# One PSUM tile for both halves in layer 0's mixers, and the ranks' diagonals written during the ranking

## The chip, the cores and the metric

The kernel runs on one core of a Trainium2 chip. The metric is the device time of one execution in microseconds, as the median of several runs; lower is better. The engines are called PE (matmuls; PEld are its weight loads), ACT, DVE, POOL and SP. The queues of SP, ACT and POOL also issue the DMA transfers; a transfer issued by SP is shown under "SPq".

## The reference

The network is a "metaformer" of four layers on a batch of 4 images of 64 channels, 128 x 128. Only two of its stages matter here.

Layer 0's mixer works on each of the 256 channel images ("tokens") on its own. Cut to what matters:

```python
an = _inorm(a, n2_g, n2_b)
h = gelu(_inorm(_spectral_conv(an, m1_spec, (H, W))) + _conv1x1(an, m1_sw, m1_sb))
h = _inorm(_spectral_conv(h, m2_spec, (H, W))) + _conv1x1(h, m2_sw, m2_sb)
o = _inorm(h, mo_g, mo_b) + a
```

`_spectral_conv` takes a two-dimensional Fourier transform, keeps 32 x 17 low modes, multiplies them by weights and transforms back; `_inorm` normalises one image. The input `a` of the mixer is itself partly made of low modes, which an earlier part of the layer has left in memory.

Layer 1's attention replaces a 128 x 128 score matrix of each of 256 tokens by a function of the rank of each score in its matrix:

```python
tau = jnp.argsort(-flat, axis=-1)
ranks = (jnp.argsort(tau, axis=-1) + 1).astype(score.dtype) / n
weights = -jnp.log(ranks).reshape(shp)
```

The score is a negated squared distance, so the matrix is symmetric and its diagonal is zero, the largest value: the diagonal's ranks are known beforehand.

## The kernel before

**Layer 0's mixers** (`l0_mixer`). 256 images are taken as 16 blocks of NB = 16 images, two groups `g` of eight blocks; up to DEEP = 3 blocks are under way at once. The steps of a block are not issued where they are written: each is a `step(engine, us, reads, writes, fn, new=..., late=...)` of a `Plan`, which knows how many buffers each name has and, at `emit`, picks the next step for each engine by the costs `us` written there. PE, ACT, DVE and POOL then run in exactly that order; SP's order is left to the framework.

A block goes three times through `inverse`, the transform from modes back to the image: once for the low modes `lo` from memory (used by `add_low`), once for the modes `o` after the first weights (`conv1`), once for those after the second (`conv2`). Between them `spectral` goes the other way (`p1`, `yl`, `p2`, `m`, `o`), and `image_stats` and `root` give the normalisations.

The modes of 16 images lie as two halves of HB = 8 images on partitions 0 to 48 and 64 to 112. `inverse` takes them in two quarters, each with four images of either half:

- `over_ky`: eight matmuls into `pa`, image by image and half by half, from 49 rows to 64 partitions and 128 columns. Each half h has a PSUM tile of its own, `pa0` and `pa1`, of which it uses partitions 64h to 64h + 63; there is one buffer of each.
- `empty`: ACT brings `pa` into the SBUF tile `gt` (two buffers), half by half. For `lo` it is one copy per half (line 923); for the other two, `scaled` (line 861) takes one activation per half and image, with a scale per partition and image (`r1` or `r2`) and a bias. A scaled quarter thus has eight activations of 64 partitions x 128 elements.
- `over_kx`: two matmuls, one per half, from the 64 partitions of `gt` to all 128 partitions of `pb0` and `pb1`, 512 columns each. In the trace each matmul of fp32 data appears as two instructions, so a quarter has 16 for `pa` and 4 for `pb`.
- DVE takes `pb` in (`add_low`, lines 967 and 982).

A block ends with the residual tiles `xt`, loaded by SP, and a store of `zz` by POOL (line 1031).

**The diagonals.** Two DRAM tensors `pk`, one per group of 128 tokens, hold the ranks: 128 x 16384 int32, 8 MiB each. Their diagonals come from a constant matrix of 16384 numbers, whose other elements are written over later. The function `diagonals` issues one DMA per group on POOL's queue, which spreads the constant over all 128 tokens. It is handed into the mixers as `aside` and is a POOL step of the second block of group 1, behind that block's `lo`.

**The ranking** (`l1_ranks`). The 8128 pairs above the diagonal are sorted by a merge network of 91 stages, for two groups of 128 tokens in turn. In the forward pass (`sort_stage`) ACT copies the lower keys, POOL subtracts, ACT takes the sign into a mask `turned`, SP writes the mask to DRAM, and DVE takes minimum and maximum of two half-stages. The pass back (`back_stage`) reads the masks and undoes the network on the positions. `finish` then writes the ranks into `pk`, 127 DMAs on SP per group (line 1565), and `l1_blocks` reads them.

Of the kernel before, what the change touches and what calls it, by code (L numbers as in the profile page):

```python
# [10 lines left out]
F32 = mybir.dt.float32  # L11
# [5 lines left out]
AF = mybir.ActivationFunctionType  # L17
# [5 lines left out]
P = 128  # L23
B, H, W, C = 4, 64, 128, 128
NI = B * H
KR = 49
# [22 lines left out]
class Plan:  # L49
# [16 lines left out]
    def step(self, engine, us, reads, writes, fn, new="", late=0.0):  # L66

        i, deps, holds = len(self.steps), set(), []
        for n in new.split():

            self.last[n] = [set(), None, set()]
            self.users.append((n, self.last[n][0]))
            holds.append(len(self.users) - 1)
            if n in self.turns:
                self.turns[n].append(holds[-1])
        for n in reads.split():
            t = self.last[n]
            t[0].add(i)
            if t[1] is not None:
                deps.add(t[1])  # L80
            t[2].add(i)
        for n in writes.split():
            t = self.last.setdefault(n, [set(), None, set()])
            t[0].add(i)
            deps |= t[2]
            if t[1] is not None:
                deps.add(t[1])
            t[1], t[2] = i, set()
        for n in new.split():
            self.last[n][0].add(i)  # L90
        deps.discard(i)
        self.steps.append((engine, us, deps, holds, fn, late))
# [190 lines left out]
    return s  # L283


def l0_conv(env, x, out, tscr, prm, cst, aside):


    nc, tc = env.nc, env.tc
    KCH = ((0, 11), (11, 22), (22, 32))  # L290
    with ExitStack() as ctx:
# [8 lines left out]
        fx = const(cp, "fx", [P, 192])  # L300
        sc = {}
# [10 lines left out]
        mix = [cp.tile([P, P], F32, name="at2_%d" % g) for g in range(2)]  # L312

        tk0 = cp.tile([P, W, C], F32, name="tk0")
# [4 lines left out]
        modes = [dram.tile([KR, 64, P], F32, name="modes%d" % g) for g in range(2)]  # L319
        with ExitStack() as mctx:  # L320
# [4 lines left out]
            psum = pool("l0ps", 2, space=PSUM)  # L325
# [113 lines left out]
            with tc.tile_pool(name="l0w", bufs=1) as wp:  # L439
# [9 lines left out]
                for k in "qkv":  # L449
                    w = wp.tile([8, 16, 9, 2], F32, name="w_" + k)  # L450
# [3 lines left out]
                for k, d, dst in (("q", dqk[0], wqk[0]), ("k", dqk[1], wqk[1])):  # L454
                    t = wp.tile([8, 2, 144], F32, name="t_" + k)
# [42 lines left out]
                t0 = wp.tile([8, 1], F32, name="t0")  # L498
# [139 lines left out]
        k = {n: const(cp, n, s) for n, s in (  # L638
            ("ex", [P, W]), ("ey", [KH, C]), ("fk", [P, 2, 2, 64]), ("gw", [KH, 32]), ("first", [P, 1]),
            ("sides", [KH, P]))}  # L640
        for n in ("m1", "m2"):
            for r in range(2):
                w = cp.tile([KH, 32], F32, name="%s_w%d" % (n, r))
# [25 lines left out]
        k["c0"] = cp.tile([P, 1], F32, name="c0")  # L669
        nc.vector.tensor_add(k["c0"], sc["an_b"], sc["mo_b"])  # L670

        l0_mixer(env, x, out, tscr, mix, modes, fx, k, sc, tk0, aside)


def l0_mixer(env, x, out, tscr, mix, modes, fx, k, sc, y0, aside):

# [5 lines left out]
    with tc.tile_pool(name="l0y", bufs=1) as yp, tc.tile_pool(name="l0m", bufs=DEEP) as sb, tc.tile_pool(name="l0s", bufs=DEEP) as sm, tc.tile_pool(  # L684
        name="l0mp", bufs=2, space=PSUM
    ) as psum, tc.tile_pool(name="l0mq", bufs=1, space=PSUM) as ps1:
        plan = Plan(dict(
            gate=DEEP, xt=3, lo=2, z=DEEP, yl=1, m=1, o=DEEP, sq=1, gt=2, p1=2, p2=1, pa=1, pb=1,
            **{n: DEEP for n in (
                "st", "d", "mu", "red", "small", "ka", "kb", "kn", "kc", "va", "knh", "v1", "r1", "b1", "ks", "r2", "g2",  # L690
                "t",
# [130 lines left out]
        def inverse(v, name, modes_of, put, put_us, reads, use, use_us, uses, writes, new=""):  # L822


            def quarter(t0):
                w = {}

                def over_ky():
                    w["pa"] = [ps1.tile([P, 4, C], F32, name="pa%d" % h) for h in range(2)]
                    for j in range(4):  # L830
                        for h in range(2):
                            q = 64 * h
                            T.matmul(
                                w["pa"][h][q : q + 64, j, :], modes_of(q, t0 + j), k["ey"][q : q + KR], start=True, stop=True
                            )

                def empty():
                    w["gt"] = sb.tile([P, 4, C], F32, name="gt", bufs=2)
                    for h in range(2):
                        put(64 * h, t0, w["gt"], w["pa"][h])  # L840

                def over_kx():
                    w["pb"] = [ps1.tile([P, 4, C], F32, name="pb%d" % h) for h in range(2)]
                    for h in range(2):
                        q = 64 * h
                        T.matmul(w["pb"][h], k["ex"][q : q + 64], w["gt"][q : q + 64], start=True, stop=True)

                step("pe", 2.0, name, "pa", over_ky, new="pa")
                step("act", put_us, "pa " + reads, "gt", empty, new="gt")
                step("pe", 3.0, "gt", "pb", over_kx, new="pb")  # L850
                for h in range(2):
                    step("dve", use_us, "pb " + uses, writes(t0), lambda h=h: use(h * HB + t0, w["pb"][h]),
                         new=new if t0 == h == 0 else "")

            for t0 in range(0, HB, 4):
                quarter(t0)

        def scaled(scale, bias):
            def put(q, t0, gt, pa):
                for j in range(4):  # L860
                    S.activation(
                        gt[q : q + 64, j, :], pa[q : q + 64, j, :], AF.Identity, bias=bias(q, t0 + j),
                        scale=scale()[q : q + 64, t0 + j : t0 + j + 1],
                    )
            return put

# [35 lines left out]
        def block(g, y, made, s0, par):  # L902
# [9 lines left out]
                    nc.sync.dma_start(v["lo"][64 * h : 64 * h + KR], modes[g][:, :, s0 + HB * h : s0 + HB * h + HB])  # L912

            step("sp", 0.2, "", "lo", load_modes, new="lo gate", late=4.0)
            if g == 1 and s0 == NB:
                step("pool", 2.0, "lo", "", aside)

            def add_low(t0, pb):
                V.tensor_add(yt[:, t0 : t0 + 4, :], yt[:, t0 : t0 + 4, :], pb)

            inverse(
                v, "lo", lambda q, t: v["lo"][q : q + KR, :, t],
                lambda q, t0, gt, pa: S.copy(gt[q : q + 64], pa[q : q + 64]), 1.2, "",
                add_low, 0.75, " ".join(made), lambda t0: "l%d" % t0,
            )
            tag1, v1 = spectral(v, lambda: yt, lambda j: "l%d" % (j % HB), "m1", 4, par)
# [36 lines left out]
            def conv1(t0, pb):  # L963
# [7 lines left out]

            inverse(
                v, "o", lambda q, t: v["o"][q : q + KR, t, :],
                scaled(lambda: v["r1"], lambda q, t: v["b1"][q : q + 64, t : t + 1]), 3.6, "r1 b1",
                conv1, 1.4, "l0 l4 ks", lambda t0: "z", new="z",
            )
            step("act", 3.4, "", "z", lambda: S.activation(v["z"], v["z"], AF.Gelu))
# [3 lines left out]
            def conv2(t0, pb):  # L981
# [3 lines left out]

            inverse(
                v, "o", lambda q, t: v["o"][q : q + KR, t, :],
                scaled(lambda: v["r2"], lambda q, t: k["b2"][q : q + 64]), 3.6, "r2",
                conv2, 0.75, "", lambda t0: "z",
            )  # L990
            tagz, var2 = image_stats(v, lambda: v["z"], 2, "z", par)
# [461 lines left out]
def l1_ranks(env, dscr, keys, pk, masks, ties, tables):  # L1453
# [9 lines left out]
    with ExitStack() as ctx:  # L1463
# [175 lines left out]
        with tc.tile_pool(name="low", bufs=2, space=PSUM) as lows, tc.tile_pool(  # L1639
            name="diff", bufs=4  # L1640
        ) as diffs, tc.manual_schedule(engines={E.Activation, E.DVE, E.Pool}):
            for i in range(ns):
                for g in range(2):
                    sort_stage(g, i)
        spare = ctx.enter_context(tc.tile_pool(name="spare", bufs=1)).tile([P, NSORT], F32, name="spare")
        for g in range(2):
            number(g, keys[g], spare)
# [1738 lines left out]
def metaformer(tc, a, out, cst):  # L3386

    with ExitStack() as ctx:
        env = Env(ctx, tc)
        nc = tc.nc  # L3390
        dp = ctx.enter_context(tc.tile_pool(name="dram", bufs=1, space=DRAM))
        state = [dp.tile([NI, W, C], F32, name="state%d" % i) for i in range(5)]
        tokens = dp.tile([NI, W, C], F32, name="tokens")
        dist = dp.tile([NI, W * W], F32, name="dist")

        pk = [dp.tile([P * W * W, 1], I32, name="pk%d" % g) for g in range(2)]
        masks = [dp.tile([P, sum(NSORT // (2 * p) * (p - k if k < p else p) for p, k in merge_network(NSORT))], I8,
                         name="masks%d" % g) for g in range(2)]
        def part(prefix):
            return {k[len(prefix) :]: v for k, v in a.items() if k.startswith(prefix)}  # L3400

        x = a["x"].rearrange("b h w c -> (b h) w c")
        f0, f2 = part("L0_ffn_"), part("L2_ffn_")

        def diagonals():
            for g in range(2):
                nc.gpsimd.dma_start(
                    pk[g][0 : P * W * W, :].rearrange("(t f) o -> t (f o)", t=P), cst["l1c_diag"].partition_broadcast(P)
                )

        l0_conv(env, x, state[0], tokens, part("L0_conv_"), cst, diagonals)
        rnn_ffn(env, state[0], state[1], f0["W"], f0["VT"], f0["gamma"], f0["beta"])
        l1_layer(
            env, state[1], state[2], dist, pk, masks, part("L1_conv_"), part("L1_ffn_"), {"rowend": cst["l1c_rowend"]}
        )
        l2_conv(env, state[2], state[3], part("L2_conv_"))
        rnn_ffn(env, state[3], state[4], f2["W"], f2["VT"], f2["gamma"], f2["beta"])
        l3_layer(env, state[4], out.rearrange("b h w c -> (b h) w c"), part("L3_conv_"), part("L3_ffn_"))
# [36 lines left out]
```

## Time and profile before

| | us |
|---|---|
| runs, median of 3 | 11948.84 |
| runs, lowest and highest | 11933.74, 11949.30 |
| the profiled execution | 11937.16 |
| its span, first to last instruction | 11935.4 |
| layer 0 before the mixers | 0 to about 500 |
| the mixers | about 500 to 1420 |
| layer 0's feed-forward part | 1420 to about 1780 |
| distances of layer 1 | 1780 to about 2045 |
| ranking, forward pass | 2045 to about 3600 |
| ranking, pass back and `finish` | to 5334 |
| the rest of layer 1, layers 2 and 3 | to the end |

The stages are cut where the first instruction of the next begins on the queue that loads for it. A "busy" time of an engine is the union of its instructions' times; the idle time before an instruction is put down to what released it. The rows of PE are modelled at their ends, so a busy PE need not be at its peak. Over the whole span DVE is busy 84%, ACT 63%, PE 61% and POOL 52%, but these are averages over stages with different limits.

### The profile page before, as it was taken

What the parts mean: (1) busy time and instruction counts of PE and PEld (TensorE: products, weight loads), DVE (VectorE), ACT (ScalarE), POOL (GpSimd) and SP (SyncE); (2) the same over time, 40 slices, a digit from 0 to 9 for tenths busy, and PEclk for the clock granted to TensorE, in tenths of its full rate; (3) what the DMA queues carried; (4) which work ended last, traced back from release to release, by engine and by line L of the source; (5) the groups of instructions that cost most, each with busy time, mean ns of one, the idle gap of its engine ahead of it and who ended that gap; (6) DMA issues with size and microseconds to landing.
All of it is one profiled execution on the core that took longest, in us unless ns stands there. A gap on an engine that the chain in (4) does not pass through costs nothing. (4 is left out here: it accounts for less than half of the span.)

```text
span 11935.4 us, 113939 instructions
## 1 busy us (share of the span) xinstructions
PE 7337.1 (61%) x33966; PEld 4454.9 (37%) x33966; DVE 10014.6 (84%) x16358; ACT 7522.4 (63%) x10863; POOL 6182.3 (52%) x5276
## 2 busy tenths in 40 slices
PE   7887796000000000009998899989999999998665
PEld 5665564000000000008886344444444444446443
DVE  7566637999999999988996899999999999996444
ACT  4255534888867777633332778777878787875332
POOL 1000016999970000002332899998999999994222
PEclk8876798555555555559999899999999999999887
DMA  4223245111111111121111343433333334333434
GB/s 139 89 43 100 63 149 140 56 57 58 58 56 54 55 54 56 49 49 42 47 45 35 129 143 140 144 135 137 135 140 139 143 138 143 139 133 117 169 131 152
DMA packets 632396, 1193.48 MB, mean 100 GB/s; under 512 B 216556, under 2 KB 433998, under 8 KB 552398
## 3 DMA queue, kind: packets, MB, share of 16 engines
q1 hardware_dynamic: 587550, 1043.02, 26.1%
q0 software_dynamic: 34656, 140.92, 3.6%
q8 instruction: 274, 4.49, 0.2%
q10 hardware_dynamic: 9552, 2.08, 0.1%
q14 instruction: 364, 2.98, 0.1%
HBM read 950.89 MB, written 251.71 MB: 101 GB/s over the span
## 5 line engine op out<-in xcount | busy, mean ns | idle before, releaser
L2717 POOL TENSOR_TENSOR gs<-hist,cc 128x512 f32<-128x512 f32 x2048 | 2576.5, 1266 | 378.9 <-DVE hist L2712 217.1
L2712 DVE TENSOR_TENSOR_SCAN hist<-da,state,bs 128x512 f32<-128x512 f32 x1984 | 2523.9, 1272 | 0.0
L2726 PE MATMUL py<-gs,ident 128*128 128x512 f32 x4096 | 2246.0, 631 | 5.1 <-DVE y L2602 3.7
L1633 PE MATMUL pt<-ident,both 128*128 128x128 f32 x6 | 2.7, 447 | 3258.0 <-DVE both L1631 3258.0
L2683 ACT ACTIVATE da<-dt,am 128x512 f32<-128x512 f32 x2048 | 1414.8, 715 | 325.6 <-DVE hist L2712 323.0
L2704 DVE TENSOR_TENSOR bs<-dx,bs 128x512 f32<-128x512 f32 x2048 | 1393.8, 681 | 187.7 <-PE bs L2690 143.0
L1509 POOL TENSOR_TENSOR diff<-key 128x2048 f32<-128x2048 f32 (+11 forms) x364 | 1383.8, 3861 | 86.8 <-DVE key L1514 75.2
L1633 PEld LDWEIGHTS pt<-ident,both 128*128 128x128 f32 x6 | 1.1, 183 | 3259.5 <-issue 3259.5
L2726 PEld LDWEIGHTS py<-gs,ident 128*128 128x128 f32 x4096 | 739.3, 197 | 902.5 <-issue 441.2
L1884 POOL IOTA row<- 72x1 int32 x1 | 0.1, 136 | 1800.7 <-ACTq L1833 1800.7
L2690 PE MATMUL bs<-bt,pick 96*128 96x512 bf16 x2048 | 807.3, 394 | 140.3 <-DVE hist L2712 137.3
L1531 ACT COPY keep<-rank 128x1536 int16<-128x1536 int16 (+11 forms) x364 | 612.8, 1686 | 437.9 <-DVE rank L1533 389.0
L1507 ACT COPY low<-key 128x2048 f32<-128x2048 f32 (+11 forms) x364 | 626.7, 1722 | 285.1 <-DVE key L1514 276.4
L1532 DVE COPY_PREDICATED rank<-back,rank 128x1536 int16<-128x1536 uint8 (+11 forms) x364 | 781.8, 2148 | 16.7 <-ACT keep L1531 16.7
L1533 DVE COPY_PREDICATED rank<-back,keep 128x1536 int16<-128x1536 uint8 (+11 forms) x364 | 778.0, 2137 | 12.5
L1514 DVE TENSOR_TENSOR key<-low,key 128x2048 f32<-128x2048 f32 (+11 forms) x364 | 744.5, 2045 | 12.4
L1513 DVE TENSOR_TENSOR key<-low,key 128x2048 f32<-128x2048 f32 (+11 forms) x364 | 749.2, 2058 | 6.5 <-DMA key<-dist 6.2
L1510 ACT ACTIVATE turned<-diff 128x2048 int8<-128x2048 f32 (+11 forms) x364 | 600.0, 1697 | 36.4 <-DMA key<-dist 27.6
L1522 ACT ACTIVATE back<-turned 128x3072 uint8<-128x3072 int8 (+12 forms) x182 | 582.3, 3200 | 0.0
L2183 PE MATMUL pe<-ew,xg 128*128 128x128 f32 x4096 | 504.4, 277 | 0.0
L1031 POOL DMA_DIRECT2D state<-zz x16 | 18.6, 1161 | 909.7 <-DVE zz L1021 854.5
L2183 PEld LDWEIGHTS pe<-ew,xg 128*128 128x128 f32 x4096 | 488.2, 193 | 3.9
(826 smaller groups left out, 18502.8 us busy)
## 6 DMA issues: line engine op xcount, KB each, us to landing
cc<-cd SPq DMA_DIRECT2D x512, 1024.0 KB
xt<-state SPq DMA_DIRECT2D x64, 1024.0 KB
xo<-state SPq DMA_DIRECT2D x128, 256.0 KB
state<-xo POOLq DMA_DIRECT2D x128, 256.0 KB, 2.8
xl<-in_L_ffn_weight SPq DMA_DIRECT2D x32, 1024.0 KB
tk<-in_x SPq DMA_DIRECT2D x32, 512.0 KB
tokens<-tt POOLq DMA_DIRECT2D x32, 512.0 KB, 5.2
tk<-tokens SPq DMA_DIRECT2D x8, 2048.0 KB
```

The lines of the kernel that those rows point to most:

```text
L1509: nc.gpsimd.tensor_sub(d, lo[part], hi[part])
L1513: nc.vector.tensor_tensor(lo[part], c, hi[part], ALU.min)
L1514: nc.vector.tensor_tensor(hi[part], c, hi[part], ALU.max)
L1532: nc.vector.copy_predicated(l, t, h)
L1533: nc.vector.copy_predicated(h, t, kv)
L2183: T.matmul(w["pe"][:, j, :], w["xg"][:, q, j, :], ew[:, q, :], start=False, stop=(j == 3 and q == E - 1))
L2683: nc.scalar.activation(da, x_["dt%d" % b], AF.Exp, scale=am[:, s : s + 1])
L2690: nc.tensor.matmul(bs, pick[:, s, :], x_["bt%d" % b], start=True, stop=True)
L2704: nc.vector.tensor_mul(db, x_["dx%d" % b], db)
L2712: nc.vector.tensor_tensor_scan(h, live.pop(("da", t)), live.pop(("db", t)), 0.0 if first else state[b][:, s : s + 1], ALU.mult, ALU.add,)
L2717: nc.gpsimd.tensor_tensor(gs, h, live.pop(("cc", t)), ALU.mult)
L2726: nc.tensor.matmul(x_["py%d" % b], env.ident, live.pop(("gs", t)), start=(s == 0), stop=(s == S - 1))
```

## The change

The two tiles `pa0`, `pa1` become one tile `pa` in a pool with two buffers: half h writes partitions 64h to 64h + 63 of the same tile. ACT empties all 128 partitions at once: one copy where there were two, four activations where there were eight. The plan is told so: `pa` has two buffers, and the costs of the four steps become smaller. The function `diagonals` and its step on POOL go away; the forward pass of the ranking issues the same bytes on SP, one piece of 1024 numbers for 128 tokens (0.5 MiB) after both groups' stages of each of 32 iterations in the middle, 16 pieces for one group and then 16 for the other.

```diff
@@ l0_mixer
-            gate=DEEP, xt=3, lo=2, z=DEEP, yl=1, m=1, o=DEEP, sq=1, gt=2, p1=2, p2=1, pa=1, pb=1,
+            gate=DEEP, xt=3, lo=2, z=DEEP, yl=1, m=1, o=DEEP, sq=1, gt=2, p1=2, p2=1, pa=2, pb=1,
...
                 def over_ky():
-                    w["pa"] = [ps1.tile([P, 4, C], F32, name="pa%d" % h) for h in range(2)]
+                    w["pa"] = psum.tile([P, 4, C], F32, name="pa")
                     for j in range(4):
                         for h in range(2):
                             q = 64 * h
                             T.matmul(
-                                w["pa"][h][q : q + 64, j, :], modes_of(q, t0 + j), k["ey"][q : q + KR], start=True, stop=True
+                                w["pa"][q : q + 64, j, :], modes_of(q, t0 + j), k["ey"][q : q + KR], start=True, stop=True
                             )
 
                 def empty():
                     w["gt"] = sb.tile([P, 4, C], F32, name="gt", bufs=2)
-                    for h in range(2):
-                        put(64 * h, t0, w["gt"], w["pa"][h])
+                    put(t0, w["gt"], w["pa"])
...
-                step("pe", 2.0, name, "pa", over_ky, new="pa")
+                step("pe", 1.3, name, "pa", over_ky, new="pa")
                 step("act", put_us, "pa " + reads, "gt", empty, new="gt")
-                step("pe", 3.0, "gt", "pb", over_kx, new="pb")
+                step("pe", 1.1, "gt", "pb", over_kx, new="pb")
...
         def scaled(scale, bias):
-            def put(q, t0, gt, pa):
+            def put(t0, gt, pa):
                 for j in range(4):
                     S.activation(
-                        gt[q : q + 64, j, :], pa[q : q + 64, j, :], AF.Identity, bias=bias(q, t0 + j),
-                        scale=scale()[q : q + 64, t0 + j : t0 + j + 1],
+                        gt[:, j, :], pa[:, j, :], AF.Identity, bias=bias(t0 + j), scale=scale()[:, t0 + j : t0 + j + 1]
                     )
...
-            if g == 1 and s0 == NB:
-                step("pool", 2.0, "lo", "", aside)
...
-                lambda q, t0, gt, pa: S.copy(gt[q : q + 64], pa[q : q + 64]), 1.2, "",
+                lambda t0, gt, pa: S.copy(gt, pa), 0.6, "",
...
-                scaled(lambda: v["r1"], lambda q, t: v["b1"][q : q + 64, t : t + 1]), 3.6, "r1 b1",
+                scaled(lambda: v["r1"], lambda t: v["b1"][:, t : t + 1]), 1.9, "r1 b1",
...
-                scaled(lambda: v["r2"], lambda q, t: k["b2"][q : q + 64]), 3.6, "r2",
+                scaled(lambda: v["r2"], lambda t: k["b2"]), 1.9, "r2",
@@ l1_ranks
             for i in range(ns):
                 for g in range(2):
                     sort_stage(g, i)
+                if ns // 2 - 16 <= i < ns // 2 + 16:
+                    g, q = divmod(i - ns // 2 + 16, 16)
+                    q *= P * W // 16
+                    nc.sync.dma_start(
+                        pk[g][0 : P * W * W, :].rearrange("(t f) o -> t (f o)", t=P)[:, q : q + P * W // 16],
+                        tables["diag"][q : q + P * W // 16].partition_broadcast(P),
+                    )
@@ metaformer
-        def diagonals():
-            for g in range(2):
-                nc.gpsimd.dma_start(
-                    pk[g][0 : P * W * W, :].rearrange("(t f) o -> t (f o)", t=P), cst["l1c_diag"].partition_broadcast(P)
-                )
-
-        l0_conv(env, x, state[0], tokens, part("L0_conv_"), cst, diagonals)
+        l0_conv(env, x, state[0], tokens, part("L0_conv_"), cst)
```

The argument `aside` goes from the functions that handed it on, and the table of the diagonals is handed to `l1_layer` instead.

More of the change, by code (lines that the diff above doesn't have):

```diff
@@ L283, in symmetrize, with l0_conv @@
     return s
-def l0_conv(env, x, out, tscr, prm, cst, aside):
+def l0_conv(env, x, out, tscr, prm, cst):
     nc, tc = env.nc, env.tc
@@ L670, in l0_conv, with l0_mixer @@
         nc.vector.tensor_add(k["c0"], sc["an_b"], sc["mo_b"])
-        l0_mixer(env, x, out, tscr, mix, modes, fx, k, sc, tk0, aside)
-def l0_mixer(env, x, out, tscr, mix, modes, fx, k, sc, y0, aside):
+        l0_mixer(env, x, out, tscr, mix, modes, fx, k, sc, tk0)
+def l0_mixer(env, x, out, tscr, mix, modes, fx, k, sc, y0):
     nc, tc = env.nc, env.tc
@@ L3403, in metaformer @@
         f0, f2 = part("L0_ffn_"), part("L2_ffn_")
-        def diagonals():
-            for g in range(2):
-                nc.gpsimd.dma_start(
-                    pk[g][0 : P * W * W, :].rearrange("(t f) o -> t (f o)", t=P), cst["l1c_diag"].partition_broadcast(P)
-                )
-        l0_conv(env, x, state[0], tokens, part("L0_conv_"), cst, diagonals)
+        l0_conv(env, x, state[0], tokens, part("L0_conv_"), cst)
         rnn_ffn(env, state[0], state[1], f0["W"], f0["VT"], f0["gamma"], f0["beta"])
         l1_layer(
-            env, state[1], state[2], dist, pk, masks, part("L1_conv_"), part("L1_ffn_"), {"rowend": cst["l1c_rowend"]}
+            env, state[1], state[2], dist, pk, masks, part("L1_conv_"), part("L1_ffn_"),
+            {"rowend": cst["l1c_rowend"], "diag": cst["l1c_diag"]},
         )
```

## The prediction

> **What bounds the kernel now.** Both halves of the change lie in stages far from each other, so I read the busy table by stage first, the waits and groups of each stage next, and single instructions last. The mixers of layer 0 run from about 500 to 1420 us. In the table of windows (columns: busy us and count of PE, weight loads, DVE, ACT, POOL, then the granted TensorE clock, DMA share, GB/s):
>
> ```profile
> 500.00:1420.00 920.00, 749.56 (x4056) 510.45 (x4055) 591.21 (x2164) 502.65 (x1172) 19.83 (x20) 0.72 0.26 66
> 2500.00:2800.00 300.00, 0.00 (x0) 0.00 (x0) 297.40 (x154) 243.88 (x154) 282.41 (x76) 0.50 0.14 57
> 940.00:960.00 20.00, 16.38 (x113) 13.23 (x113) 11.24 (x39) 10.73 (x28) 2.26 (x3) 0.84 0.87 236
> 960.00:980.00 20.00, 15.70 (x78) 8.12 (x74) 15.53 (x65) 7.86 (x23) 0.00 (x0) 0.67 1.04 332
> 980.00:1000.00 20.00, 18.61 (x90) 12.38 (x90) 9.38 (x32) 16.42 (x35) 0.00 (x0) 0.62 0.93 283
> ```
>
> The mixers are paced by PE: busy 750 of 920 us, no other engine over 65%. The ranking's forward pass (second line) is paced by DVE, 297 of 300 us, with the DMA engines at 14%. The last three lines are the flood of the diagonals, 16.8 MB from 949 us on.
>
> Then the waits of the mixers (engine, line, releaser: total us, times, longest), and the groups kept apart by shape:
>
> ```profile
> PEld pb L846 <- ACT gt L861: 94.2, 85, 2.9
> PE pb L846 <- ACT gt L861: 41.8, 47, 2.8
> PE pa L833 <- DVE o L802: 38.1, 13, 4.1
> L861 ACT ACTIVATE gt<-pa,b,r 64x128 f32<-64x128 f32 x512 | 191.0, 448 | 82.4 <-PE pa L833 72.3 <-DVE r L711 4.9 <-DVE r L961 3.4
> L923 ACT COPY gt<-pa 64x512 f32<-64x512 f32 x64 | 37.1, 580 | 21.8 <-PE pa L833 20.7
> ```
>
> What PE waits for most is ACT emptying `pa`. The cost is larger than the wait, as four lines of the timeline show (start, length, engine, then idle before):
>
> ```profile
> 809.03 1.97 PE L833 MATMUL pa<-ey,o 49*64 49x128 f32 x16
> 811.08 3.01 ACT L861 ACTIVATE gt<-pa,b,r 64x128 f32<-64x128 f32 x8 [3.78 <-PE pa L833]
> 812.62 3.59 PE L846 MATMUL pb<-gt,ex 64*128 64x512 f32 x4 [1.63 <-ACT gt L861]
> 799.95 2.08 PE L846 MATMUL pb<-gt,ex 64*128 64x512 f32 x4
> ```
>
> The first half's four activations release the first two `pb` matmuls at 812.62; the other two must wait 1.5 us for the second half's, and the four take 3.59 us. Where both halves were ready (799.95) the same four take 2.08 us, because the two 64-row halves run side by side.
>
> Last, the diagonals: DVE waits for a residual tile whose load is behind the flood.
>
> ```profile
> 1012.54 1.14 DVE L1008 SCALAR_TENSOR_TENSOR xt<-tk,ka,xt 128x128 f32<-128x128 f32 x4 [17.87 <-DMA xt<-in_x]
> L3407 POOL DMA_DIRECT2D pk<-in_l1c_diag x2: 545/556/566, 949.2 to 949.8; - x2
> 16.19 0.37 SPq L297 DMA_DIRECT2D ex<-in_l0c_ex  x1
> ```
>
> **What the Trainium skill says.** "TensorE: Matmul & The Clock Gate", Part 3 (packing small matmuls): matmuls on different row and column tiles of the array run concurrently. The trace agrees: the sixteen quarter-array `pa` matmuls took 1.09 us at 1344.76 where sixteen whole-array ones of the same width (`p` from `fx`, 1068.69) took 2.02. The same page, Part 1: the array's clock falls to half after some microseconds of idling; the trace shows 0.5 to 1.0 granted, and `pb` at 1.13 or 2.08 us for the same four. "PSUM — Partial Sum Buffer", the section on bank collisions: column tiles may write one bank at once on disjoint partitions; different row tiles may not share a bank at once, which is then narrowed to the same 32-partition quadrant by measurement. The new `pa` differs in both. The trace shows column tiles alone doing it: `p2` writes both halves into one bank, and its sixteen 256-wide matmuls took 2.46 us at 1064.75, about twice the 1.13 us of the four 512-wide `pb`, which are paired and have half the columns. "DMA: Bandwidth & Descriptors", on issuing engines: all queues share sixteen DMA engines and interleave; the 17.87 us above is that.
>
> **The change part by part.**
>
> *Fewer activations.* Per scaled quarter, eight 64x128 become four 128x128, each copy two 64x512 become one 128x512. The nearest row: partitions don't lengthen an ACT instruction (a 128x256 from PSUM takes 467 ns at L2625, a 128x512 copy about 580). So ACT sheds (191 + 37)/2 = 114 us, worth nothing by itself, since ACT is busy 503 of 920.
>
> *Its effect on PE.* A scaled quarter's `gt` is whole when the old first half was, so `pb` starts when it did and runs at 2.08 rather than 3.59: 1.51 us. In the timeline's `pb` rows 33 of 64 scaled quarters show 3.59, 8 more are split in two with a wait between (about as much): 41 x 1.51 = 62 us. Of the 32 plain quarters 12 show 2.67 instead of 2.07: 7 us. Sum 69. The others had cover (PE had other work), and gain nothing.
>
> *Two buffers of `pa`* (the bank count stays: two banks before, two after). The second quarter's `pa`, 1.97 us, can go into the idle time before the first quarter's `pb`. That is at most the 41.8 + 8.6 us of PE waits; the repeating pattern 1.63 + 0.68 us a block, in some 13 blocks, gives 30.
>
> *The planner's costs.* A quarter's PE steps fall from 5.0 to 2.4 us. Summing the planner's costs over one block, PE falls from 48.6 to 33 and DVE, 44, becomes what it orders by; before, PE's 48.6 stood beside a measured 54 us from one block to the next (the 3.59 us row at 1103.58 and its like at 1158.33 and 1211.43). Real DVE work is about 591/920 of that, 35 us, so DVE doesn't bind, but the order changes and some of the gain will turn into waits on DVE such as `o` (38.1 us now). I take 80% of 69 + 30: **80 us**, some 6 us a block from 54 to 48. Bounds: 20, where the order eats most of it, and 160, where a block comes near PE's own work, 54 x 750/920 = 44 less 5 for the pairs, and the clock rises with it.
>
> *The diagonals leave layer 0.* POOL loses two issues (1.1 us) between two stores, of no weight. The stall goes: DVE stood 17.87 us for that load, and a wait of 4.35 came before it. What it cost is read from the stores of `zz`: those at 948.08 and 1016.04 are 68.0 us apart, against 53 to 55 around them, so **13 us**, bounds 10 and 22 (both waits in full). The residual load is then on time; what is late next is ACT's last scaling, as in other blocks.
>
> *They arrive in the ranking.* 32 pieces of 0.5 MB, each about 2 us of the DMA engines at the 236 to 332 GB/s above, 65 us in all, over some 560 us at a share of 14%. On SP 32 issues of some 0.4 us, 13 us, on a queue that waits 1350.8 us there for ACT's `turned`. Behind them in SP's queue stand the mask stores; their release is needed only three masks later, some 25 us. Cover: DVE at 99%. **0 us**, bounds 0 and 10. The later rank writes into `pk` (254 on SP at 5175 to 5323) now follow SP's own transfers instead of POOL's, long landed: 0, bounds -2 and 5.
>
> Sum: -80 - 13 + 0 = -93 from the profiled execution's 11937.2 (span 11935.4 and 1.8 around it) is 11844. The runs shown have a median of 11948.8 and reach down to 11933.7; the profiled one is near their lower end, so I add 6: **11850 us**.
>
> **Rivals.**
>
> *The pieces don't stay in the ranking.* SP's order isn't written out by hand; the last line of the last fence shows a constant asked for after the attention going out at 16.19 us, half a millisecond ahead of its place. The pieces need nothing in SBUF and wait for nothing, so they could go out at the start too. There 20 MB move in 120 us; 16.8 more at about 300 GB/s makes 124 us of transfers: cost between 0 and 56, take 30. Against it: the loads seen that early are of the same stage. Time 11880. Chance 0.25.
>
> *The gain becomes another wait.* The new order leaves PE waiting for `o`, `red` or the gelu; half or less of the 80 comes, say 35: 11895. For: those waits sum to over 70 us now. Against: DVE has a third of its time free. Chance 0.12.
>
> *Slower: one bank makes the two halves' `pa` matmuls take turns.* Then sixteen take as long as unpaired ones: 0.96 us more at full clock, 1.9 at half; 96 quarters x 1.4 = 137, less 93, +44: 11937 + 6 + 44 = 11987. It decides from 93/96 = 0.97 us a group on. For: the skill's sentence on row tiles. Against: the halves are in different quadrants, and `p2` pairs in one bank. Chance 0.08.
>
> **How the numbers follow.** My forecast has 0.55. About 0.2%, 24 us, is what a measurement can tell from no change. Faster: 0.55 + 0.25 and a bit under half of the third case, 0.84; same 0.07; slower 0.09, the bank and a little for an order that turns out badly. The range runs from the upper bounds of both gains, nearly (160 + 13 is 11770), to the early flood at its full 56 with 70% of the gain in order (11925); outside are the bank and a few extremes.
>
> **What would show it.** L861 256 times at 128x128 near 450 ns; `pb` in fours at 1.1 to 2.1 us without 3.59; stores of `zz` 47 to 49 us apart and no stall near 949; PE's waits for `gt` under half. The pieces on SP between about 2400 and 3100 us with DVE still at 99%. I am wrong if `pa` groups of sixteen last over 3 us, if the pieces show in the first 100 us, or if PE's waits for DVE grow by what the waits for ACT lose.

## The result and the profile after

| | before | after |
|---|---|---|
| median of 5 runs each, us | 11948.84 | 11887.27 |
| lowest and highest, us | 11932.91, 11949.59 | 11861.20, 11917.43 |
| the profiled execution, us | 11937.16 | 11887.27 |

The ratio after/before is 0.9954, with a 95% interval from 0.9937 to 0.9971: about 61 us less by the medians, 50 us less by the profiled executions. The forecast was 93 less. So the sign and the range held, and between half and two thirds of the gain came: the forecast's own ratio, 11850 to the 11943 that it started from, is 0.9922, which lies below the measured interval.

The table of windows of the kernel after shows the mixers and the ranking (columns as before: busy us and count of PE, weight loads, DVE, ACT, POOL, then clock, DMA share, GB/s):

```profile
500.00:1420.00 920.00, 674.72 (x4315) 501.94 (x4315) 618.23 (x2302) 413.64 (x944) 26.53 (x37) 0.77 0.22 54
2500.00:2800.00 300.00, 0.00 (x0) 0.00 (x0) 297.47 (x149) 244.44 (x149) 286.36 (x75) 0.50 0.14 58
```

PE's busy time in the mixers' window fell from 750 to 675 us and ACT's from 503 to 414. But the mixers end only some 47 us sooner, so the window of the kernel after holds some 50 us of the next stage too: PE shed more work than the time did. In the ranking the DMA share and the throughput stand where they stood. That is the first surprise, since 32 pieces were to pass there.

The waits of the mixers (engine, what it waited in, releaser: total us, times, longest) name the second surprise:

```profile
PEld pb L844 <- ACT gt L859: 73.2, 25, 14.7
PE pb L844 <- ACT gt L859: 66.5, 16, 14.5
PE pa L832 <- DVE o L801: 32.3, 9, 4.9
```

PE's wait for `gt` was to halve. It grew from 41.8 to 66.5 us, in a third of the times: 47 short waits, 2.8 us at most, became 16, one of them 14.5 us long. The groups kept apart by shape show that the merging itself did what the diff says:

```profile
L859 ACT ACTIVATE gt<-pa,b,r 128x128 f32<-128x128 f32 x256 | 94.8, 464 | 57.2 <-PE pb L844 28.8 <-DVE r L956 19.9 <-DVE r L710 8.6
L844 PE MATMUL pb<-gt,ex 64*128 64x512 f32 x384 | 173.9, 811 | 88.3 <-ACT gt L859 66.5 <-DVE zz L962 14.3 <-DVE zz L977 5.7
```

Before, the second of these rows read:

```profile
L846 PE MATMUL pb<-gt,ex 64*128 64x512 f32 x384 | 233.6, 923 | 51.5 <-ACT gt L861 41.8 <-ACT gt L923 8.6 <-DVE kn L942 1.1
```

There are half as many activations, each 464 ns where a half took 448, and `pb` keeps PE busy for 174 us where it was 234: 60 us of PE gone.

For what follows, a stage table helps. It is read from single rows: the last store of `modes` by POOL (the end of what stands before the mixers), and the first and last store of `zz` after it.

| kernel | `modes` end | first `zz` store | last `zz` store | mixers (last store less `modes` end) |
|---|---|---|---|---|
| before | 484.9 | 618.4 | 1413.6 | 928.8 |
| after | 493.1 | 672.6 | 1366.2 | 873.1 |

The 49.9 us of the profiled executions are 55.7 from the mixers, less 8.2 lost ahead of them, and 2.4 over the rest of the program.

### The profile page after: what moved, and what is told of

Its sections match the earlier page's. It is cut to its first block, busy times and chain, and to the rows that moved or that the text cites. A ratio compares the mean times of both kernels' runs of the same rounds, so it can differ in the third digit from the quotient of the medians.

```text
span 11885.4 us, 113599 instructions
## 1 busy us (share of the span) xinstructions
PE 7219.7 (61%) x33966; PEld 4411.3 (37%) x33966; DVE 10015.2 (84%) x16358; ACT 7406.1 (62%) x10575; POOL 6180.0 (52%) x5274
## 3 DMA queue, kind: packets, MB, share of 16 engines
q8 instruction: 273, 4.47, 0.2%
q10 hardware_dynamic: 9552, 2.08, 0.1%
```

## The experiments

Each time is compared with the kernel before as it was measured beside it, since the median of before alone went from 11919 to 11949 us. A mixers' time comes from one profiled execution. Where two kernels have the same order in the mixers and no flood there, these times differ by 3 us (after and the fourth run) and 5 us (third and ninth), and the fifth run lies 13 us from the sum of its parts; so a single step of 10 us or less is not read from them.

**First: the merged tile alone, in the old order.** The costs stay as before, the plan counts one buffer of `pa`, and the diagonals stay on POOL. (`pa=1` or `pa=2` is what the plan reckons with; the pool of the merged tile has two buffers in every run.) In the traces PE and DVE then run the same instructions in the same order as before in the mixers. Against the kernel after, beside the diagonals:

```diff
-  pa=2, pb=1,
+  pa=1, pb=1,
-  step("pe", 1.3, name, "pa", over_ky, new="pa")
+  step("pe", 2.0, name, "pa", over_ky, new="pa")
-  step("pe", 1.1, "gt", "pb", over_kx, new="pb")
+  step("pe", 3.0, "gt", "pb", over_kx, new="pb")
-  lambda t0, gt, pa: S.copy(gt, pa), 0.6, "",
+  lambda t0, gt, pa: S.copy(gt, pa), 1.2, "",
-  scaled(lambda: v["r1"], lambda t: v["b1"][:, t : t + 1]), 1.9, "r1 b1",
+  scaled(lambda: v["r1"], lambda t: v["b1"][:, t : t + 1]), 3.6, "r1 b1",
-  scaled(lambda: v["r2"], lambda t: k["b2"]), 1.9, "r2",
+  scaled(lambda: v["r2"], lambda t: k["b2"]), 3.6, "r2",
```

> The mixers with the one tile of both halves, but with the buffers of pa (one) and the planner's costs of before, so every engine's order of instructions is that of before; the diagonals stay on POOL in the mixers. Theory A (merging the halves by itself makes pb run in pairs, the planner's new order then cost part of it): the 41 + 12 quarters with a wait between the halves lose it, 50 to 69 us off, 11880 to 11900. Theory B (the order gives the gain, merging alone nothing, since PE finds the same waits for r1 and o): under 20 us off, above 11925.

Measured: 11849.75 against 11919.22, 69.5 us less, ratio 0.9938 [0.9925, 0.9951]. The mixers take 857.5 us, 71.3 less than before. The first theory holds: merging alone, with nothing in the order moved, brings more than the whole change does. It isn't PE's waits that fall (those for `gt` stand at 40.6 us, before 41.8) but the time of the `pb` matmuls, from 233.6 to 171.8 us.

**Second: the changed mixers, the diagonals where they were.** The kernel after with `diagonals` on POOL in the mixers' step again.

```diff
-  (32 pieces on SP in l1_ranks)
+  if g == 1 and s0 == NB:
+      step("pool", 2.0, "lo", "", aside)
```

> The changed mixers, with the diagonals on POOL in the second block of group 1 as before. Theory A (the early diagonals cost layer 0's front 8 us, and the flood in the mixers 13): 5 us above the changed kernel, about 11892, the stage before the mixers ending near 485 us as before. Rival (the early pieces cost 30, as my prediction had it): about 20 below the changed kernel.

Measured: 11912.69 against 11919.22, ratio 0.9993 [0.9984, 1.0001]: 6.5 us less, and no difference that can be told. Both theories missed: the one expected a gain 5 us below that of the change, the other a larger one, and the change's gain of 61 us was almost wholly gone. The mixers take 900.4 us. The timeline shows that the flood is dearer in the new order:

```profile
1005.71 1.14 DVE L1005 SCALAR_TENSOR_TENSOR xt<-tk,ka,xt 128x128 f32<-128x128 f32 x4 [32.85 <-DMA xt<-in_x]
```

DVE is idle for 32.85 us until the residual tile is there, where it was 17.87 before and, with the merged tile in the old order (the first run), 17.41. The same mixers without the flood (the fourth run) take 24 us less.

**Third: the diagonals alone.** The mixers of before, the 32 pieces on SP.

```diff
-  if g == 1 and s0 == NB:
-      step("pool", 2.0, "lo", "", aside)
...
+  if ns // 2 - 16 <= i < ns // 2 + 16:
+      nc.sync.dma_start(pk[g]..., tables["diag"][q : q + P * W // 16].partition_broadcast(P))
```

> The mixers of before, the diagonals in 32 pieces on SP as in the changed kernel. Theory A: the pieces go out from about 37 us on, the front ends 8 us later, the flood's 13 us go: 5 us below the kernel before, within noise of it. Rival (front costs 30): 15 above it.

Measured: 11916.47 against 11919.22, ratio 0.9995 [0.9987, 1.0003]: 2.8 us less, not to be told from none. In the stages two terms nearly cancel: the mixers take 914.0 us, 14.8 less than before, and the stage ahead of them ends 11.9 us later, at 496.7.

**Fourth: the pieces held behind their mask store.** The kernel after, with each piece queued behind the store of its iteration on SP.

```diff
-  nc.sync.dma_start(masks[g][...], m[...])
+  stored = nc.sync.dma_start(masks[g][...], m[...])
...
+  with tc.issue_after(stored.ins):
       nc.sync.dma_start(pk[g]..., tables["diag"][...].partition_broadcast(P))
```

> The changed kernel with each piece held in SP's queue behind the mask store of its iteration, so that the pieces do go out in the ranking's forward pass. Theory A (DVE covers them there): the front ends near 485 us again, DVE stays at 99% in the ranking, 8 us below the changed kernel, about 11880. Rival (they delay the mask stores or the transfers the ranking needs): the ranking's forward pass longer than the changed kernel's by 10 us or more, no gain or a loss.

Measured: 11875.33 against 11919.22, ratio 0.9961 [0.9946, 0.9976]. The rows of the pieces in the trace, first in the kernel after (durations min/median/max in ns, first and last start in us):

```profile
L1643 SPq DMA_DIRECT2D pk<-in_l1c_diag x32: 500/596/1310, 37.3 to 149.8; - x32
```

and in this run:

```profile
L1645 SPq DMA_DIRECT2D pk<-in_l1c_diag x32: 496/496/628, 2464.3 to 2964.6; - x32
```

In the kernel after, the pieces written in the middle of the ranking went out in the first 150 us. A window over that time shows what they did there, before and then after:

```profile
40.00:150.00 110.00, 79.11 (x405) 62.84 (x404) 79.80 (x466) 48.65 (x159) 12.43 (x14) 0.84 0.51 170
```

```profile
40.00:150.00 110.00, 79.11 (x380) 63.63 (x376) 80.09 (x465) 48.25 (x159) 12.42 (x14) 0.81 0.89 302
```

The DMA engines were half idle there and took nearly all of the pieces: share 0.51 to 0.89, while the engines' busy times hardly move. The layer's first part ended 8.2 us later, at 493.1. With the pieces anchored it ends at 484.2, where it ended before. These 8 us are little more than the spread of that figure: in the nine profiled kernels without early pieces the first part ends between 484.2 and 491.2 us, 487.4 on average, and in the two with them at 493.1 and 496.7. So the early pieces cost some 6 to 9 us there. What they cost in the ranking is nearly nothing, though the DMA engines are now seen to carry them:

```profile
2450.00:2750.00 300.00, 0.00 (x0) 0.00 (x0) 297.40 (x154) 244.02 (x154) 282.20 (x76) 0.50 0.27 89
```

DVE is as busy as before, and the pass from ACT's first `turned` to its first `back` takes 1479.1 us against 1478.3 before. By their ratios to before, this run and the kernel after can't be told apart.

**Fifth: both parts, old order, pieces anchored.** The first run's mixers with the fourth run's pieces; against the first run:

```diff
-  if g == 1 and s0 == NB:
-      step("pool", 2.0, "lo", "", aside)
...
+  with tc.issue_after(stored.ins):
+      nc.sync.dma_start(pk[g]..., tables["diag"][...].partition_broadcast(P))
```

> The merged tile in the order of before (one buffer of pa, the costs of before) as in e1, and the pieces of the diagonals held in the ranking as in e4: PE, ACT and DVE run e1's lists to the instruction. Theory A (the two gains add: 69 by the merging, 14 for the flood that e1 still has between its stores at 909.62 and 973.11): mixers 843 us from the last store of modes to the last store of zz, 83 below the kernel before. Rival (the flood's stall covered other waits, which come back): mixers 855 or more, 70 or less below.

Measured: 11832.95 (11825.34 to 11840.67) against 11925.73, 92.8 us less, ratio 0.9927 [0.9913, 0.9941]: the fastest of all. The mixers take 830.2 us, 43 less than in the kernel after and some 13 less than expected. The gains of the parts at least add up; against the first run, taking the flood away brought 27 us, where 14 were expected. The mixers of this run differ from the fourth run's only in the planner's costs and in the buffers that the plan counts: they are the same instructions in another order. The waits of this run, to be set against those of the kernel after:

```profile
PE pb L844 <- ACT gt L859: 40.4, 41, 2.9
PE pa L832 <- DVE o L801: 31.7, 13, 3.4
```

No wait of these two kinds is over 3.4 us, where the new order had one of 14.5.

**Sixth and seventh: the two buffers alone, the costs alone.** Which of the two spoils the order? The sixth is the fifth with `pa=2`; the seventh is the fourth with `pa=1`, that is, the fifth with the new costs.

```diff
# sixth, against the fifth
-  pa=1, pb=1,
+  pa=2, pb=1,
# seventh, against the fourth
-  pa=2, pb=1,
+  pa=1, pb=1,
```

> As e5, but with two buffers of pa, so that the planner orders anew by the costs of before. Theory C (the costs of PE, set below what the trace shows, spoiled the order; the second buffer is worth the idle PE time before pb): mixers 820 to 840. Theory D (the second buffer spoiled it, since the planner issues pa ahead of work that others wait for): mixers 865 to 880, as in e4.

> As e4, but with one buffer of pa: the costs of the change, the buffer of before. Theory C (the costs spoiled the order): mixers 865 to 885, the first store of zz near 665 us as in e4. Theory D (the buffer did): mixers 840 to 850 as in e5, the first store near 616.

Measured: the sixth 11848.81 (0.9939 [0.9925, 0.9953]), mixers 839.8; the seventh 11863.20 (0.9954 [0.9939, 0.9968]), mixers 852.1. Against the fifth's 830.2 the second buffer costs 9.6 us and the new costs 21.9; both together (the fourth, 876.4) cost 46.2, more than the two added. The 9.6 alone is no more than the spread of such figures, but with the new costs the second buffer costs 24.3 us (fourth against seventh), and in whole times five of the sixth's six executions lie above the slowest of the fifth's. So the second buffer brings no gain under either set of costs. The sixth falls in the band of the theory that blames the costs, at its upper edge, and the seventh just above the band of the one that blames the buffers: neither theory holds alone, and each had part of it. In the sixth, PE's waits for `gt` do fall, as the extra buffer was to bring:

```profile
PE pb L844 <- ACT gt L859: 31.4, 8, 6.2
PE pa L832 <- DVE o L801: 57.6, 21, 7.4
```

40.4 to 31.4 us; but those for `o` from DVE rise from 31.7 to 57.6.

**Eighth: costs for PE nearer to what PE takes.** The fourth with 1.6 and 1.7 us in place of 1.3 and 1.1; in the trace of the kernel after a quarter's `pa` takes 1.84 us and its `pb` 2.08 at the half clock, 1.13 at the full one.

```diff
-  step("pe", 1.3, name, "pa", over_ky, new="pa")
+  step("pe", 1.6, name, "pa", over_ky, new="pa")
-  step("pe", 1.1, "gt", "pb", over_kx, new="pb")
+  step("pe", 1.7, "gt", "pb", over_kx, new="pb")
```

> As e4, but with PE's two costs of a quarter set to what the trace shows on the average, 1.6 and 1.7 us, in place of 1.3 and 1.1. Theory C: the order recovers at least half, mixers below 860. Rival (the order turns on ACT's smaller costs or on chance): mixers within 10 of e4's 876.

Measured: 11846.66 against 11925.73, 79 us less, ratio 0.9943 [0.9927, 0.9959]; mixers 847.0. Two numbers that issue no instruction and change none, and 29 of the 46 us are back. The mixers of the fourth to the eighth run issue the same instructions, so what one of them loses against another lies in their order. The 17 us between this run and the fifth were not divided between ACT's lower costs and the second buffer.

**Ninth: is it the pairing, or the tile?** The fifth, but the one tile is emptied half by half, as the two were; the plain quarters' copies are split in the same way.

```diff
-  for j in range(4):
-      S.activation(gt[:, j, :], pa[:, j, :], ...)
+  for q in (0, 64):
+      for j in range(4):
+          S.activation(gt[q : q + 64, j, :], pa[q : q + 64, j, :], ...)
```

> The order and costs of before, one buffer of the one-tile `pa`, the pieces behind their mask store (the kernel of the fifth run), but `pa` is emptied half by half as before: eight activations of 64 partitions a scaled quarter, two copies a plain one. Theory A (the gain of the first part is the pairing of `pb`, which needs both halves of `gt` at one moment): it goes; the 3.59 us rows of `pb` are back, the mixers take about the 928.8 us of before less the 14 of the flood, 905 to 925, and the time is 10 to 20 us under before. Theory B (the gain lies in the tile itself, one PSUM tile in place of two): the mixers stay at 830 to 860 and the time 75 to 95 us under before.

Measured: 11919.68 against 11927.18, ratio 0.9990 [0.9983, 0.9997], 7.5 us less where 10 to 20 were expected; mixers 908.6. The first theory holds: the rows of `pb` with 3.59 us are back, 33 as before, where the fifth has none. A quarter in this run's timeline:

```profile
809.63 3.01 ACT L860 ACTIVATE gt<-pa,b,r 64x128 f32<-64x128 f32 x8 [3.08 <-PE pa L832]
811.18 3.59 PE L844 MATMUL pb<-gt,ex 64*128 64x512 f32 x4 [1.65 <-ACT gt L860]
```

and its like in the fifth:

```profile
784.47 1.51 ACT L859 ACTIVATE gt<-pa,b,r 128x128 f32<-128x128 f32 x4 [1.87 <-PE pa L832]
786.03 2.08 PE L844 MATMUL pb<-gt,ex 64*128 64x512 f32 x4 [1.66 <-ACT gt L859]
```

In both, `pb` starts 1.55 us after ACT did, having waited 1.65. Half by half it then takes 3.59 us, its second pair waiting for ACT's second four; emptied whole, 2.08. The tile alone brings nothing that can be seen: the mixers of this run and of the third, with two tiles, are 5 us apart. The 908.6 - 830.2 = 78.4 us lie in the emptying. They show in PE's own time: an instruction of `pb` lasts 917 ns on average in this run and 871 in the fifth, but the 384 of them keep PE busy for 234.6 us here and 170.8 there, because there they overlap in pairs. PE's waits for `gt` hardly differ, 42.6 us and 40.4. So some 64 of the 78 us are the pairs themselves. PE's busy time in the mixers falls by 77 us in all, 759.0 to 681.6; the other 13 go along with a higher granted clock, 0.73 here and 0.77 there, and were not followed further.

## Why the prediction was right or wrong

From the mixers of before to those of the change the runs make a chain: 928.8, less 20.2 for the flood (ninth), less 78.4 for the pairs (fifth), plus 46.2 for costs and buffers (fourth), is 876.4. It closes by the way it is built; the kernel after, with the same order, has 873.1.

| step | forecast, us | measured, us | from |
|---|---|---|---|
| pairs of `pb` | -69 | -71 and -78 | first; fifth against ninth |
| two buffers of `pa` | -30 | +10; +24 with the new costs | sixth against fifth; fourth against seventh |
| the new costs, and both together | +19 (the fifth that was taken off 99) | +22, and +46 with the buffers | seventh, fourth against fifth |
| the flood leaves layer 0 | -13 | -15, -20, -27; -24 in the new order | third; ninth; fifth against first; fourth against second |
| 32 pieces | 0, in the ranking | +8 and +12, at the start (+6 and +9 against the average) | kernel after; third |

**The pairs were right**, in mechanism and size. Counting the 3.59 us rows and taking 1.51 us from each was enough; where a `pb` had cover before, little more was to be got. The ninth run shows it by emptying in halves again and changing nothing else.

**The two buffers are the step that failed**: forecast at -30 us, they brought none of it and under the new costs lost 24. The argument was that a second quarter's `pa` fits into PE's idle time before the first quarter's `pb`. It does fit: in the timeline of the kernel after, both quarters' 32 matmuls run in one go.

```profile
812.66 3.68 PE L832 MATMUL pa<-ey,o 49*64 49x128 f32 x32 [4.47 <-DVE o L801]
821.47 1.00 PE L745 MATMUL stat<-d,half_w 128*128 128x16 f32 x4 [0.83 <-DVE d L737]
829.07 2.90 ACT L859 ACTIVATE gt<-pa,b,r 128x128 f32<-128x128 f32 x8 [1.62 <-DVE r L956]
830.63 2.08 PE L844 MATMUL pb<-gt,ex 64*128 64x512 f32 x4 [8.15 <-ACT gt L859]
```

But what ACT needs is not only `pa`. Its activation waits for `r`, DVE's last step of a normalisation; DVE comes to it after a run of more than thirty small operations, which the `stat` matmuls at 821.47 release. From the end of those, 822.47, to 830.63 PE has nothing in its order that can run, 8 us; at 683.01 the same row has 14.55 us before it. The wait is put down to ACT, whose own part is the last 1.55 us; behind it is DVE, with operations of about 0.2 us one after the other. In the fifth run, the old order, no wait for `gt` is longer than 2.9 us, so there other work of PE lay over that chain. The prediction looked at which engine had idle time, and not at what the longest chain of a block was and what covered it.

**The planner's costs were mis-sized.** The prediction saw that the new costs make DVE the engine that the plan orders by, and allowed a fifth of the gain for it. With the buffers it took 46. The argument against more was that DVE's real work doesn't bind; in busy time it doesn't, 618 of 920 us, but a chain through DVE does. Nor does the reason given, that DVE's planned 44 us a block now exceed PE's, decide it: with the eighth run's costs PE's planned sum is 33 + 6 x 0.9 = 38.4 us (six quarters at 3.3 us in place of 2.4), still below 44, and most of the loss is gone. Where in the run the loss falls: the sixth store of `zz` stands 401 us after the last store of `modes`, and before 409, so six blocks gained only 8; the other ten come every 47.2 us, (1366.16 - 894.48)/10, where the forecast said 47 to 49. In the fifth run the sixth stands 375 us after it, and the others come every 45.5. How the planner comes from its costs to this order was not followed step by step; that the order is what costs is shown by the fourth to the eighth run.

**The flood** was somewhat larger than read off one gap between stores: 15 to 27 us against 13, where the bounds were 10 and 22.

**The place of the pieces is the first rival's**, to which the prediction gave a quarter: SP's order is not written out, and a transfer that waits for nothing went to the start. The pieces in the first 100 us were also one of the prediction's own signs of being wrong. Their price was 6 to 12 us where 30 were taken, since most of what they moved, 302 GB/s against 170 in the window, went through DMA engines that had been idle. The rival's time, 11880, lies close to the result, but by chance: it took too much for the pieces and nothing more for the order. This also falsifies "arrive in the ranking: 0" as a statement on the kernel as it stands; as a statement on the ranking it held (fourth run: 0.8 us, DVE at 99%).

**The second rival**, the gain becoming other waits, came true for about half of the gain, but not through the waits that it named: in the kernel after the waits for `o` are 32.3 us (before 38.1) and those for `red` 24.5 (19.5). What grew is the wait for `gt`, behind the normalisation. **The third**, halves taking turns in one bank, is refuted: two groups of sixteen took 3.68 us at the half clock, 1.84 each, against 1.97 with two banks before. The Trainium skill, "TensorEngine Tiling (Array Packing)", Gotcha 1, says that different row tiles can't use one PSUM bank at once; at these tiles, with rows and output partitions 0 to 63 for one half and 64 to 127 for the other, this trace doesn't show such a limit.

The total stayed in the range because its upper end allowed for an order that keeps part of the gain and for the early flood, and both came. (That end is a sum that comes to 11943 + 56 - 0.7 x 93 = 11934 us, not 11925; it changes nothing.) Some luck was in it: the flood and the pairs gave more than forecast, and so took back part of what the order lost.

**A better version** came of it: the fifth run, the change without its new costs and its second buffer, and with the pieces held at their place. Its median is 11832.95 us, 0.9927 [0.9913, 0.9941] of before, where the change has 0.9954 [0.9937, 0.9971]; the intervals just overlap, so the whole times alone don't tell the two apart for certain; the stages do, by the 43 us of the mixers.

## What to carry to other kernels

Two half-array matmuls (here `pb`: 2.08 us together, 3.59 apart) share their time only when both inputs are ready together, so what feeds such a pair should be released by one instruction, or by two that end together; count the rows where the pair takes the longer time to estimate the gain. When an edit makes steps cheaper in a planned order, measure it first in the old order, and treat the new costs and extra buffers as an edit of their own. A transfer that waits for nothing is placed by whoever orders its queue: tie it to a neighbour if its place matters, and look up where it went.

## What the runs showed of the hardware that was not expected

Some 17 MB from DRAM to DRAM, put beside loads that held half of the DMA engines' time, raised the throughput from 170 to 302 GB/s over 110 us and delayed the stage by only some 6 to 12 us. The Trainium skill, "DMA: Bandwidth & Descriptors", in its section on issuing engines, says that all queues share the sixteen engines. The windows above don't test it, since pieces and loads were both on SP. The mixers agree with it: the flood was on POOL's queue and the residual load on SP's, and DVE was idle for 17.87 us until that load was there, where without the flood (third run) the waits for such loads around that place are 4.3 us. The same 16.8 MB in two transfers made DVE idle for 17.41 us with the merged tile in the old order (first run) and for 32.85 in the new one (second run): the order of the instructions decided.

PE's granted clock over the 30 us with the 8 us wait (812 to 842) was 0.50, against 0.77 over the mixers, and the four `pb` after that wait took 2.08 us and not 1.13. But the wait did not bring the clock down: it was 1.00 from 809 to 812, while PE was idle for 4.47 us, and 0.53 from 812 to 816, before the 8 us began. Over the mixers as a whole it is 0.77 in the fourth run and 0.77 in the fifth, so the 46 us between them are not a matter of the clock.
